# Routing of a mixture of experts emitted among the next step's attention, with four expert tiles left over from step to step

## The chip, the cores and the metric

The kernel runs on one core of a Trainium2 chip. The core has a matrix engine (TensorE, PE below), three engines for elementwise work (VectorE, DVE; ScalarE, ACT; GpSimd, POOL), a queue engine that here only starts transfers (SyncE, SP), and 16 DMA engines. Each engine works through its own list of instructions in order, and an instruction that has to wait holds everything behind it on that engine. The metric is the time of one execution on the device, in microseconds.

## The reference

Two layers over an image of 2 x 56 x 56 positions with 256 channels, all in float32.

- Layer 0: group norm, then attention of every position over its 7 x 7 neighbourhood (8 heads), added to the input.
- Layer 1: layer norm, then a linear attention along the 3136 tokens of each image with running sums, added; then layer norm and a mixture of 8 experts, of which each token uses two, added.

The part that matters here, in short:

```python
t = t + _L1_attn_ref(_ln_t(t), ...)
xf = _ln_t(t).reshape(-1, 256)
probs = softmax(xf @ gate_w + gate_b)              # 8 experts
top2_vals, top2_idx = top_k(probs, 2)              # weights of the two best
for e in range(8):
    h = gelu(xf @ W1[e] + b1[e])                   # 256 -> 512
    y = h @ W2[e] + b2[e]                          # 512 -> 256
    t = t + cw[:, e] * y                           # cw is 0 unless e is among the two best
```

## The kernel before

Layer 0 takes the first 485 us and is not touched. Layer 1 walks over the tokens in 14 steps (`NST`), each of 448 tokens: 224 of each image, as four blocks of 112. For every step `s` there are three sequences of work, written as Python generators that emit a few instructions and then yield. One yield is called a turn.

- `before_pairs(s)` loads the step's tokens into `x`, normalises and transposes them (`norm_T`), projects q, k and v and makes the rows of gates and softmax weights. Its scans and four reciprocals on 16 x 224 values are DVE work.
- `attention(s)` makes the running sums: `p_gt` is its first matmul, `sc`, `zz` and `po` the core, `p_out` the last projection, and the result is added to `x`. In the kernel before it ends with `route(s, x)`.
- `route` normalises `x` into `xs` and transposes it (`pt_x` from `xs`), multiplies by the gate weights (`p_gate`), takes softmax and the rank of each expert on DVE, and writes `taken`. After that come six empty turns (`PAUSE`). Then `p_n` counts the tokens of each expert with two small matmuls; DVE makes the row numbers `rowi`; POOL writes the tokens to their experts' regions in `xs_d` in device memory with eight indirect transfers (scatters), each after the one before. `listed(s)` writes the list of full tiles. Last, `p_cw` and `p_b` add the experts' output biases to `x`, and POOL writes `x` to `out`.

Besides these runs one generator `experts()` for the whole layer. A tile is 256 tokens of one expert. `fetch` reads the tile's list entry on SP and loads its tokens (`xg`, from `xs_d`) and the expert's weights (`wj`, 1 MB), two tiles ahead (`ahead = 2`). `gather` transposes the tokens (`pt_g`), `hidden` makes 512 hidden values (`p_h`, then gelu on ACT), and `results` multiplies back (`p_y`), scales (`ye`), and adds the rows into `out` with an indirect transfer that accumulates. The rows' numbers come from a cast of a column of `xg` (`rows_e`). A tile takes `per_tile` = 7 turns; there are 56 (`NX`). `sure(s)` is the number of tiles that are full after step `s` whatever the input: 0, 0, 3, 7, 10, 14, 17 and so on to 42.

`together(main, *others)` sets the order: after every turn of the main generator it takes as many turns of the others as keep them at their share of the main one's expected turns. The main one is `attention(s)`, routing included (47 turns); the others are the tiles that the step before made sure, less two, and `before_pairs(s + 1)`. After the last step two more tiles run, then the list is closed, and the remaining 18 tiles run alone.

The instructions of each engine follow this order closely; a scheduler moves some of them forward, among them loads on SP and the cast `rows_e`. Data in device memory is tracked by tensor: a fetch waits for the scatters emitted before it, a scatter for the fetches before it, and an accumulation into `out` for the one before.

Matmul results go to PSUM; pool `l_mm` has six buffers that all these products share. `x`, `xs`, `xg` and `wj` come from pool `p3` with three buffers each, `ye` and `rows_e` from `p6` with six. `general` is a second form of the layer for other inputs, which does not run here.

Of the kernel before, what the change touches and what calls it, by code (L numbers as in the profile page):

```python
# [14 lines left out]
F32 = mybir.dt.float32  # L15
# [12 lines left out]
C = 256  # L28
# [12 lines left out]
TT = 112  # L41
BLK = 448
BT = BLK // NB
NST = L // BT
NTI = BLK // TT
# [12 lines left out]
NX = (2 * NB * L - NE) // SL + NE  # L58
TOK, CWC = C, C + 1
ROW = C + 16  # L60
PAUSE = 6


def sure(s):

    return max(0, -((NE * (SL - 1) - 2 * BLK * (s + 1)) // SL))
# [88 lines left out]
def hybrid_kernel(ctx: ExitStack, tc: tile.TileContext, t: dict, out: bass.AP):  # L155
# [170 lines left out]
    with (  # L326
# [36 lines left out]
        for n in range(2):  # L363
            o = p1.tile([TT, 2, NH, HD + 1], F32, name=f"values{n}")
# [169 lines left out]
        for i in range(NT):  # L534
            going, done = project(i + 2) if i + 2 < NT else iter(()), 0
# [103 lines left out]
    def layer_1(general):  # L639
        with (  # L640
# [3 lines left out]
            p1 = steps.enter_context(tc.tile_pool(name="l1", bufs=1))  # L644
            p2 = steps.enter_context(tc.tile_pool(name="l2", bufs=2))
            p3 = steps.enter_context(tc.tile_pool(name="l3", bufs=2 if general else 3))
            p6 = steps.enter_context(tc.tile_pool(name="l6", bufs=2 if general else 6))
            ps_a = steps.enter_context(tc.tile_pool(name="l_acc", bufs=1, space=PSUM))

# [75 lines left out]
            def before_pairs(s):  # L725

                nonlocal m_prev, s_prev, g_prev
                x = p3.tile([TT, NTI, C], F32, tag="x", name="x_acc")
                for b in range(NB):
                    nc.sync.dma_start(  # L730
                        out=x[:, b * 2 : (b + 1) * 2, :],
# [48 lines left out]
                at = 0  # L780
# [187 lines left out]
            def attention(s):  # L968
                x, q, k, v, gl, cf = ready.pop(s)
                yield from (sums_general if general else sums_plain)(s, q, k, v, gl, cf)  # L970

                for i in range(NTI):
                    ps = ps_m.tile([TT, C], F32, tag="mm", name="p_out")
                    for g in range(NG):
                        nc.tensor.matmul(
                            ps,
                            lhsT=q[:, g, i * TT : (i + 1) * TT],
                            rhs=wo1[:, g, :],
                            start=g == 0,
                            stop=g == NG - 1,  # L980
                        )
                    nc.vector.tensor_tensor(x[:, i, :], ps, x[:, i, :], ALU.add)
                    yield
                yield from route(s, x)

            def sums_general(s, q, k, v, gl, cf):

# [154 lines left out]
                    nc.vector.tensor_tensor(qg, spread(cf, g, rep), own, ALU.mult)  # L1142
                    yield

            def route(s, x):


                nonlocal n_prev, c_prev, at_prev
                xs = p3.tile([TT, NTI, ROW], F32, tag="xs", name="xs")
                nc.gpsimd.memset(xs[:, :, CWC + NE :], 0.0)  # L1150
                xT = yield from norm_T(x, "xT_f", p1, xs)
# [29 lines left out]
                ahead = p1.tile(full, F32, tag="ahead", name="ahead")  # L1181
# [22 lines left out]

                taken = p2.tile([TT, NTI, NE], F32, tag="taken", name="taken")
                nc.vector.tensor_single_scalar(taken, rank, 1.5, ALU.is_lt)  # L1206
                for _ in range(PAUSE):
                    yield
                pn = ps_m.tile([P, 2, NTI, NE], F32, tag="mm", name="p_n")
                flat = taken.rearrange("p i e -> p (i e)")  # L1210
                nc.tensor.matmul(  # L1211
# [9 lines left out]
                n = p2.tile([P, NTI + 1, NE], F32, tag="n", name="n")  # L1221
# [131 lines left out]
            def fetch(j):  # L1353

                ent, k = listed_at.pop(j)
                known = "the lists hold rows of the regions and experts alone"
                row = nc.values_load(
                    ent[0:1, 0, k : k + 1],
                    engines=[mybir.EngineType.SP],
                    min_val=0,  # L1360
                    max_val=NE * RG,
                    skip_runtime_bounds_check_because=known,
                )
                exp = nc.values_load(
                    ent[0:1, 1, k : k + 1],
                    engines=[mybir.EngineType.SP],
                    min_val=0,
                    max_val=NE - 1,
                    skip_runtime_bounds_check_because=known,
                )  # L1370
                xg = p3.tile([P, SL // P, ROW], F32, tag="xg", name="xg")
                nc.sync.dma_start(
                    out=xg, in_=xs_d[bass.ds(row, SL), :].rearrange("(u p) c -> p u c", p=P)
                )
                wj = p3.tile([P, NG * FF + NF * C + NF], F32, tag="wj", name="wj")
                nc.sync.dma_start(
                    out=wj, in_=t["we"][bass.ds(exp, 1)].rearrange("o p c -> (o p) c")
                )
                return xg, wj

            def gather(xg):

                pt = ps_h.tile([P, NG, SL], F32, tag="mm", name="pt_g")
                for u in range(SL // P):
                    for g in range(NG):
                        nc.tensor.transpose(  # L1386
                            pt[:, g, u * P : (u + 1) * P], xg[:, u, g * P : (g + 1) * P], ident
                        )
                xT = p2.tile([P, NG, SL], F32, tag="xT_g", name="xT_g")
                nc.scalar.copy(xT, pt)  # L1390
                return xT

            def hidden(xT, wj):
                w1 = wj[:, : NG * FF].rearrange("p (k f) -> p k f", k=NG)
                b1 = wj[:, NG * FF + NF * C :]
                hT = p2.tile([P, NF, SL], F32, tag="hT", name="hT")
                for f in range(NF):
                    ph = ps_h.tile([P, SL], F32, tag="mm", name="p_h")
                    for k in range(NG):
                        nc.tensor.matmul(  # L1400
                            ph,
                            lhsT=w1[:, k, f * P : (f + 1) * P],
                            rhs=xT[:, k, :],
                            start=k == 0,
                            stop=k == NG - 1,
                        )
                    nc.scalar.activation(hT[:, f, :], ph, AF.Gelu, bias=b1[:, f : f + 1])  # L1407
                    yield
                return hT
# [41 lines left out]
            def experts():  # L1451


                fetched = {k: fetch(k) for k in range(ahead)}
                yield
                xT = gather(fetched[0][0])
                for k in range(NX):
                    if k + ahead < NX:
                        fetched[k + ahead] = fetch(k + ahead)
                    xg, wj = fetched.pop(k)  # L1460
                    hT = yield from hidden(xT, wj)
                    if k + 1 < NX:
                        xT = gather(fetched[k + 1][0])
                    yield
                    yield from results(k, hT, xg, wj)
# [8 lines left out]
            def together(main, *others):  # L1474


                going = [[gen, n, 0, wait * main[1]] for gen, n, wait in others]
                for done, _ in enumerate(main[0], 1):
                    for o in going:
                        while o[2] < o[1] and o[2] * (main[1] - o[3]) < (done - o[3]) * o[1]:  # L1480
                            next(o[0], 0)
                            o[2] += 1
                for gen, n, at, _ in going:
                    for _ in range(at, n):
                        next(gen, 0)
                return done
# [1 line left out]

            ready, listed_at = {}, {}
            ahead = 1 if general else 2
            tiles = experts()
            per_tile = NF + 1 + SL // P
            n_before = sum(1 for _ in before_pairs(0)) + 1
            n_step = 70
            for s in range(NST):
                n_tiles = max(0, sure(s - 1) - ahead) - max(0, sure(s - 2) - ahead)
                begin = n_tiles and sure(s - 2) <= ahead
                if begin:  # L1500
                    next(tiles)
                with_it = [(tiles, n_tiles * per_tile, 0.5 if begin else 0)]
                if s + 1 < NST:
                    with_it.append((before_pairs(s + 1), n_before, 0))
                n_step = together((attention(s), n_step), *with_it)
            for _ in range(ahead * per_tile):
                next(tiles)


            behind = p1.tile([P, NE], I32, tag="behind", name="behind")  # L1510
# [21 lines left out]
    with tc.If(flag != 0):  # L1532
        layer_1(False)
    with tc.If(flag == 0):  # L1534
        layer_1(True)
# [56 lines left out]
```

## Time and profile before

The median of three runs is 1860.25 us (1853.78 to 1864.68). The profile is of one execution of 1865.8 us.

| stretch | us | what runs |
|---|---|---|
| 0 to 515.3 | 515.3 | layer 0 and the first `before_pairs` |
| 515.3 to 697.7 | 182.4 | steps 0 to 2, no tiles |
| 697.7 to 770.3 | 72.6 | step 3, one tile |
| 770.3 to 1548.4 | 778.1 | steps 4 to 12, 32 tiles |
| 1548.4 to 1590.3 | 41.9 | attention of step 13 |
| 1590.3 to 1640.3 | 50.0 | routing of step 13, tiles |
| 1640.3 to 1865.8 | 225.5 | last tiles |

A step is cut here from one `p_gt` on PE to the next. In the timeline each line has the start, the time from the first start to the last end of the merged instructions, engine, line, operation, output and inputs, and how many (a float32 matmul shows as two). What stands in square brackets is the idle time of the engine just before and the instruction that ended it. A line of the windows has the stretch, its length, then busy time and number of instructions of PE, PE's weight loads, DVE, ACT and POOL, the clock granted to PE, the busy share of the DMA engines and GB/s.

### The profile page before, as it was taken

Reading aid. Unit: us, or ns where it says so; the run is one execution under the profiler, and the core shown is the slowest. Engines: PE = TensorE matmul, PEld = TensorE weight load, DVE = VectorE, ACT = ScalarE, POOL = GpSimd, SP = SyncE. Lnnn points to the kernel's source line nnn. Section 1 sums busy time; section 2 is a strip of 40 time slices with the busy share of each in tenths; the row PEclk is TensorE's granted clock in tenths of the full one; section 3 lists DMA queues with packets and bytes.
Section 4 is the critical chain, followed back from the end, with each engine's and each line's share of the span. In section 5 each row is a group of like instructions: output and inputs, shape, how many; then the busy total and the mean of one; then the engine's idle time right before and its main releaser. Section 6 shows DMA issues by size and latency. Waiting matters only on the chain. (4 is left out here: it accounts for less than half of the span.)

```text
span 1865.8 us, 28574 instructions
## 1 busy us (share of the span) xinstructions
PE 1504.1 (81%) x10840; PEld 1075.6 (58%) x10840; DVE 936.4 (50%) x2787; ACT 626.3 (34%) x1125; POOL 448.5 (24%) x496
## 2 busy tenths in 40 slices
PE   0899999999487778898798879888887888778781
PEld 0466776789254445565465556556565656666670
DVE  3455566654466775655637373746465464411110
ACT  0233433432333233443325333433344241322220
POOL 2123333332101101213131322213131313322232
PEclk9989999975688779899899989898899899989885
DMA  7345554452101103234242414232333324276542
GB/s 227 119 147 168 161 152 145 150 164 85 41 1 41 31 11 127 47 107 109 61 115 63 116 45 126 62 92 71 106 75 98 105 61 109 65 238 170 137 106 27
DMA packets 110786, 190.35 MB, mean 102 GB/s; under 512 B 17674, under 2 KB 92290, under 8 KB 103460
## 3 DMA queue, kind: packets, MB, share of 16 engines
q1 hardware_dynamic: 74612, 128.27, 21.7%
q0 software_dynamic: 32560, 54.55, 13.2%
q10 hardware_dynamic: 3456, 5.51, 0.9%
q8 instruction: 89, 1.46, 0.3%
q14 instruction: 69, 0.57, 0.1%
HBM read 131.52 MB, written 56.73 MB: 101 GB/s over the span
## 5 line engine op out<-in xcount | busy, mean ns | idle before, releaser
L1440 POOL DMA_INDIRECT out<-ye,rows_e x112 | 175.3, 1565 | 635.7 <-DVE ye L1439 206.8
L1400 PE MATMUL p_h<-xT_g,wj 128*128 128x256 f32 x896 | 242.1, 411 | 14.0 <-DVE ye L1439 9.6
L1431 PE MATMUL p_y<-wj,hT 128*128 128x256 f32 x896 | 230.8, 409 | 1.1 <-DVE ye L1439 1.1
L1407 ACT ACTIVATE hT<-p_h,wj 128x256 f32<-128x256 f32 x224 | 105.7, 474 | 351.2 <-PE p_h L1400 317.2
L1400 PEld LDWEIGHTS p_h<-xT_g,wj 128*128 128x128 f32 x896 | 175.8, 204 | 52.6 <-issue 18.2
L1431 PEld LDWEIGHTS p_y<-wj,hT 128*128 128x128 f32 x896 | 178.0, 206 | 38.4 <-issue 9.5
L1246 POOL DMA_INDIRECT xs_d<-xs,rowi x112 | 107.6, 961 | 321.6 <-DMA xs_d<-xs,rowi 129.5
L503 ACT ACTIVATE ex<-ex 98x1024 f32<-98x1024 f32 x98 | 103.8, 1060 | 228.0 <-DVE ex L497 219.2
L1415 DVE CAST rows_e<-xg 128x2 int32<-128x2 f32 x56 | 9.5, 169 | 301.2 <-DMA xg<-xs_d 202.6
L497 DVE TENSOR_TENSOR ex<-sc,bias 98x1024 f32<-98x1024 f32 x98 | 119.7, 1221 | 66.9 <-PE sc L488 65.3
L512 PE MATMUL po<-vw,ex 98*64 98x33 f32 x3136 | 129.2, 240 | 5.8 <-DMA vw<-v_d 5.8
L512 PEld LDWEIGHTS po<-vw,ex 98*64 98x64 f32 x3136 | 117.2, 157 | 23.7 <-DMA vw<-v_d 7.1
L488 PE MATMUL sc<-qb,kc 64*98 64x128 f32 x1568 | 130.0, 311 | 0.0
L488 PEld LDWEIGHTS sc<-qb,kc 64*98 64x98 f32 x1568 | 106.0, 187 | 40.5 <-issue 28.6
L916 PE MATMUL sc<-qh,v 128*112 128x448 f32 x224 | 112.3, 598 | 0.0
L924 DVE TENSOR_TENSOR qv<-sc,upto 112x448 f32<-112x448 f32 x112 | 69.2, 622 | 72.1 <-PE sc L916 70.7
L1439 DVE TENSOR_SCALAR ye<-p_y,cws 128x256 f32<-128x256 f32 x112 | 52.6, 478 | 80.8 <-PE p_y L1431 57.3
L1211 PE MATMUL p_n<-taken,every 112*128 112x32 f32 x28 | 8.2, 383 | 89.9 <-DVE taken L1206 89.9
L315 POOL TENSOR_TENSOR xo<-xo,xq 128x256 f32<-128x256 f32 x49 | 35.6, 727 | 181.4 <-DVE xo L309 173.3
L1386 PE MATMUL pt_g<-ident,xg 128*128 128x128 f32 x224 | 39.4, 304 | 41.1 <-DVE ye L1439 26.2
L954 PE MATMUL po<-qv,kt 112*32 112x112 f32 x896 | 45.7, 277 | 30.9 <-DVE qv L924 30.9
L888 ACT COPY qh<-q 32x448 f32<-32x448 f32 x112 | 63.0, 562 | 2.2
(234 smaller groups left out, 2543.3 us busy)
## 6 DMA issues: line engine op xcount, KB each, us to landing
wj<-in_we SPq DMA_DIRECT2D x56, 1026.0 KB
vw<-v_d SPq DMA_DIRECT2D x196, 101.1 KB
xg<-xs_d SPq DMA_DIRECT2D x56, 272.0 KB
v_d<-values POOLq DMA_DIRECT2D x28, 231.0 KB, 3.7
xq<-in_x SPq DMA_DIRECT2D x98, 64.0 KB
q_d<-evq POOLq DMA_DIRECT2D x28, 224.0 KB, 3.0
qb<-q_d SPq DMA_DIRECT2D x56, 112.0 KB
x_d<-xo POOLq DMA_DIRECT2D x98, 64.0 KB, 3.1
```

Of the source, the lines that this page charges most:

```text
L488: nc.tensor.matmul(sc[:KN, p, b, k], lhsT=keys(i, j, k, b, rows, g), rhs=qb[rows, g, :, b, j * QN : (j + 1) * QN], start=True, stop=True,)
L497: nc.vector.tensor_tensor(ex[:KN], sc[:KN].rearrange("n p b k h q -> n p b (k h q)"), tables[kind][:KN, g].unsqueeze(2).to_broadcast(wide) ...
L503: nc.scalar.activation(ex[:KN], ex[:KN], AF.Exp)
L512: nc.tensor.matmul(po[b * QN : (b + 1) * QN, hh, :], lhsT=ex[:KN, p, b, k, h, :], rhs=vw[:KN, b, k, hh * (HD + 1) : (hh + 1) * (HD + 1)], ...
L888: nc.scalar.copy(qh[hp, h, :], qg[hp])
L916: nc.tensor.matmul(sc, lhsT=vg[:, i * TT : (i + 1) * TT], rhs=qh[:, :, i * TT : (i + 1) * TT], start=True, stop=True,)
L924: nc.vector.tensor_tensor(qv, sc, upto.unsqueeze(1).to_broadcast([TT, 4, TT]), ALU.mult)
L1246: nc.gpsimd.indirect_dma_start(out=xs_d[:, :], out_offset=bass.IndirectOffsetOnAxis(ap=rowi[:, c, i : i + 1].bitcast(U32), axis=0), in_=xs ...
L1400: nc.tensor.matmul(ph, lhsT=w1[:, k, f * P : (f + 1) * P], rhs=xT[:, k, :], start=k == 0, stop=k == NG - 1,)
L1407: nc.scalar.activation(hT[:, f, :], ph, AF.Gelu, bias=b1[:, f : f + 1])
L1431: nc.tensor.matmul(py, lhsT=hT[:, f, u * P : (u + 1) * P], rhs=w2[:, f, :], start=f == 0, stop=f == NF - 1,)
L1440: nc.gpsimd.indirect_dma_start(out=out[:, :], out_offset=bass.IndirectOffsetOnAxis(ap=rows[:, u : u + 1].bitcast(U32), axis=0), in_=y, in_ ...
```

## The change

Routing becomes a sequence of its own. `attention(s)` now ends with the last addition to `x` (27 turns) and leaves `x` in `routed`; during step `s + 1`, `together` takes the 17 turns of `route(s)` over the first 0.6 of the attention's turns. Of the six empty turns one is left. Its purpose is to have the routing's chain through DVE run beside attention, not after it.

As the list of step `s` is now written during step `s + 1`, four tiles (`wait`) and not two are left over from step to step, so that a tile is not fetched before it is listed. The look-ahead of fetches stays at two. The first tile starts in step 4 and not in step 3. After the last step, routing of step 13 is the main sequence and the four tiles left run beside it, spread over 1.5 times its turns. `x` gets a pool of its own with three buffers. Lines after the first change are shifted by up to six in the changed kernel: `p_n` is at L1213, `rows_e` at L1417, `p_h` at L1402, the accumulation at L1442.

```diff
-PAUSE = 6
...
+            p4 = steps.enter_context(tc.tile_pool(name="l4", bufs=2 if general else 3))
...
-                x = p3.tile([TT, NTI, C], F32, tag="x", name="x_acc")
+                x = p4.tile([TT, NTI, C], F32, tag="x", name="x_acc")
...
-                yield from route(s, x)
+                routed[s] = x
+                if general:
+                    yield from route(s)
...
-            def route(s, x):
+            def route(s):
...
+                x = routed.pop(s)
...
-                for _ in range(PAUSE):
-                    yield
+                yield
...
-                going = [[gen, n, 0, wait * main[1]] for gen, n, wait in others]
-                for done, _ in enumerate(main[0], 1):
+                going = [[gen, n, 0, a * main[1], b * main[1]] for gen, n, a, b in others]
+                done = 0
+                for _ in main[0]:
+                    done += 1
                     for o in going:
-                        while o[2] < o[1] and o[2] * (main[1] - o[3]) < (done - o[3]) * o[1]:
+                        while o[2] < o[1] and o[2] * (o[4] - o[3]) < (done - o[3]) * o[1]:
...
+            wait = 1 if general else 4
...
-            n_step = 70
+            n_step, n_route = 45, 17
             for s in range(NST):
-                n_tiles = max(0, sure(s - 1) - ahead) - max(0, sure(s - 2) - ahead)
-                begin = n_tiles and sure(s - 2) <= ahead
-                if begin:
-                    next(tiles)
-                with_it = [(tiles, n_tiles * per_tile, 0.5 if begin else 0)]
+                n_tiles = max(0, sure(s - 1) - wait) - max(0, sure(s - 2) - wait)
+                begin = n_tiles and sure(s - 2) <= wait
+                with_it = []
+                if s and not general:
+                    with_it.append((route(s - 1), n_route, 0, 0.6))
                 if s + 1 < NST:
-                    with_it.append((before_pairs(s + 1), n_before, 0))
+                    with_it.append((before_pairs(s + 1), n_before, 0, 1))
+                with_it.append((tiles, n_tiles * per_tile + (begin > 0), 0.5 if begin else 0, 1))
                 n_step = together((attention(s), n_step), *with_it)
-            for _ in range(ahead * per_tile):
-                next(tiles)
+            together((() if general else route(NST - 1), n_route), (tiles, wait * per_tile, 0, 1.5))
```

## The prediction

> **What bounds the kernel now.** I read the engine table first, then the windows cut at the step boundaries, then the waits of TensorE (PE), and last the timelines around each wait. The chain of waits is little help: it covers the last 9% of the span.
>
> The table of engines names one engine that could be the bound, PE; VectorE (DVE) is at half.
>
> ```profile
> PE 1504.1 (81%) x10840; PEld 1075.6 (58%) x10840; DVE 936.4 (50%) x2787; ACT 626.3 (34%) x1125; POOL 448.5 (24%) x496
> ```
>
> Layer 1 begins its first attention at 515.3 us (first `p_gt`), and each later `p_gt` starts a step. A window from one `p_gt` to the next gives (length, then PE busy, PE weight loads, DVE) for step 1, with no expert tile, and steps 4 and 5, with four and three:
>
> ```profile
> 577.90:637.40 59.50, 46.07 (x263) 28.74 (x264) 41.61 (x121) 19.95 (x36) 3.94 (x5) 0.84 0.03 9
> ...
> 770.30:855.10 84.80, 76.17 (x407) 52.51 (x406) 49.43 (x180) 35.71 (x61) 21.97 (x20) 0.94 0.35 98
> 855.10:941.90 86.80, 69.88 (x373) 48.55 (x371) 47.40 (x162) 29.76 (x53) 19.58 (x18) 0.88 0.30 80
> ```
>
> Steps 4 to 12 last 778.1 us and keep PE busy for 663.0, so PE stands 115, or 12.8 a step; a step without tiles stands 13 to 15. The routing makes most of that. Its group of the page, and the timeline of PE in one step:
>
> ```profile
> L1211 PE MATMUL p_n<-taken,every 112*128 112x32 f32 x28 | 8.2, 383 | 89.9 <-DVE taken L1206 89.9
> ```
>
> ```profile
> 1430.75 0.32 PE L718 MATMUL pt_x<-ident,xs 112*128 112x112 f32 x1 [1.43 <-DVE xs L707]
> ...
> 1436.63 1.65 PE L1155 MATMUL p_gate<-gw,xT_f 128*112 128x8 f32 x16
> 1438.13 2.84 PE L1400 MATMUL p_h<-xT_g,wj 128*128 128x256 f32 x12
> 1449.40 0.64 PE L1211 MATMUL p_n<-taken,every 112*128 112x32 f32 x2 [8.44 <-DVE taken L1206]
> ...
> 1450.23 2.05 PE L1400 MATMUL p_h<-xT_g,wj 128*128 128x256 f32 x4
> ```
>
> From the gate's end (1438.1) to `p_n` DVE needs 11.3 us; PE has 2.8 us of other work queued ahead of `p_n`, then stands 8.44 and runs the next `p_h` x4 in 2.05 instead of 1.03. In the other kind of step 5.7 us of 10.5 are filled and 4.4 to 4.6 stand. Mean over 14 steps: 89.9/14 = 6.4.
>
> The other waits in a step are `pt_x` on the normalised tokens (1.43 or 2.61, 32.2 in all), `p_b` (0.6), and `po` on `qv` and `p_h` on `ye` (30.9 and 9.6 in all). The last two come from DVE itself being held:
>
> ```profile
> 1307.37 0.41 SPq L1372 DMA_DIRECT2D xg<-xs_d  x1
> ```
>
> ```profile
> 1310.78 0.17 DVE L1415 CAST rows_e<-xg 128x2 int32<-128x2 f32 x1 [10.39 <-DMA xg<-xs_d]
> ```
>
> The eight scatters of the routing run one after another from 1281.2 to 1307.4, the next fetch `xg` waits for them, and a small cast that reads it stands in DVE's order ahead of attention.
>
> Tail: after step 13's attention (1590.3) 275.5 us follow. PE waits at 1640.3 for the fetch of tile 38, which needs the last scatter (issued 1634.5); from there 38 serial accumulations into `out` take 5.5 us each to the end, against 3.7 us of PE for half a tile (7.34 a tile, 1670.28 to 1677.62).
>
> ```profile
> 1640.26 1.09 PE L1386 MATMUL pt_g<-ident,xg 128*128 128x128 f32 x4 [11.86 <-DMA xg<-xs_d]
> ```
>
> **What the skill says.** The Trainium skill, "Perfetto Trace Analysis", section "Optimization Strategy", advises to interleave stretches with different limits and to find what each gap on the bounding engine waits for; the change does the first, and the lines above are the second. "TensorE: Matmul & The Clock Gate", section "What's actually happening", says that about 3.4 us of idleness halves PE's clock for about as long. The trace agrees: after the 8.44 us gap 2.05 against 1.03 us. So a gap over some 4 us costs about 2 more, inside "busy".
>
> **The change, part by part.** The order of instructions of both kernels, which the build fixes, tells what lies between a producer and its wait.
>
> *The routing of step s moves into step s+1.* Nothing is added to PE: routing is 7 us of it (transposes 1.7, gate 1.65, `p_n` 0.7, `p_cw` 0.55, `p_b` 2.3). The waits change:
> - `p_n`. In the new order DVE has, between gate and `taken`, the 14 routing operations (3.5 us together by their rows), Exp with its table load (1.5), two `qv` (0.62 each) and in one kind of step a `ye` (0.48), but none of the 1.53 us reciprocals that `before_pairs` puts there now: 6.7, with latencies about 7.7. PE has queued ahead of `p_n`: 2 `p_h`, 2 `sc`, a transpose group, `zz` and `po` (6.4 us), or the same with a `p_y` and a `pt_g` in place of one `p_h` (7.9). Left: 0 to 1.5, I take 1. Dropping five of six pauses costs nothing for that reason.
> - `pt_x`. It now stands at the head of the step: behind the last `p_out` only a `p_y` and `p_gt` (2.5 us), or `p_gt` alone (0.6). The chain is 4.3 to 4.6 us now (last `p_out` 1426.5 or 1513.7 to `pt_x`); DVE has the next step's statistics mixed in (two to four of 0.42 us), so about 6. Left: 3.5 and 5.4, mean 4.5, up from 2.
> - Scatters and fetch. In a three-tile step the fetch needs all eight scatters: 3 us from `p_n` to `rowi`, 26 for the scatters (as now) plus about 2.5 for accumulations queued between them, 3.4 for the fetch: 35 after `p_n`, where PE has 33 us of work before DVE meets the cast. In a four-tile step a first fetch comes after two scatters, the third scatter waits for it to land, and the cast for the second fetch is ready about 43 us after `p_n` (3 to `rowi`, 9 for two scatters and the accumulation between them, 5 for that fetch, 21 for six scatters and one accumulation, 5 to land and fetch) while PE has 28 and, with six PSUM buffers, some 7 more. Left: 1 and 7, mean 4, as now (40.5 us over ten steps). Behind the cast stand `qv`, the `x_acc` additions and `q`; PE waits for them when its buffers are full.
> - `p_b` 0.6, as now. Sum of idleness a step: 4.5 + 1 + 4 + 0.6 = 10.
>
> *Busy time.* PE's 663.0 us in steps 4 to 12 less 32 tiles of 7.34 (235) is 47.6 a step; with one long gap fewer I take 46.
>
> *Four tiles left over.* With `sure()` = 3, 7, 10, 14 ... tiles start in step 4 rather than 3; steps 4 to 12 hold 31 instead of 32, step 13 three, four run with routing 13. The tail of 18 tiles and its accumulations stay. The new order of Pool's queue keeps four or five accumulations among the last eight scatters, and tile 38's transposes still stand ahead of tile 37's results: those 50 us are bound by scatter and fetch, as now, and the extra tile work lies in PE's 11.86 us gap. I add 3.
>
> *The separate pool for `x`* keeps three buffers: nothing. The load of `x` still waits for the output of three steps before; its new place, late in the step before its use, leaves about 8 us.
>
> Sum, before to after:
> - step 0: 62.6 to 47.5 (routing gone, 7 of PE and 8 of waits): -15
> - steps 1, 2: 59.9 each to 57 (46.6 + 10): -6
> - step 3: 72.6 to 57 (no tile): -15.5
> - steps 4 to 12: 778.1 to 9 x 46 + 31 x 7.34 + 90 = 731.5: -46.5
> - step 13 to its last `p_out`: 41.9 to 23.5 + 7 + 22 + 10 = 62.5: +20.5
> - rest: +3
>
> -59.5, so 1860.25 - 59.5 = **1801 us**.
>
> **Rivals.**
> 1. *All waits hidden.* DVE's queue order is kinder than my sums and 5 us a step stand: 13 steps x 5 = 65 less, 1736. For: DVE is busy only 48 of 86 us. Against: `pt_x` has little work ahead in every step.
> 2. *The wait only moves.* `p_n` goes, but `pt_x` and the casts grow to 14 a step: 13 x 4 = 52 back, 1853. For: `pt_x` and scatter are chains through several engines, untouched.
> 3. *Slower.* In every step with tiles the cast holds DVE for the whole 43 - 28 = 15 us and PE with it, `pt_x` stays at 5: 20 a step with the rest, 10 more than mine in ten steps: 1901. Against: six PSUM buffers, and now 10.4 us of held DVE cost PE only 2 to 5.
> 4. *Tail-bound:* if accumulation already limited the steps, a shorter step would return in the tail. Seven accumulations of 4.5 and eight scatters of 2.9 us are 55 of 75 us: small, counted under 2.
>
> **Chances.** My forecast 0.63; rival 1 0.15; rivals 2 and 4 0.12; rival 3 0.10. The idleness of 10 could be 7 or 13: 39 either way. The range leaves out most of 3 and the far half of 1: 1742 to 1856. Faster by over 0.5% (below 1851): 0.63 + 0.15 + 0.03 = 0.81; within: 0.08; slower: 0.11.
>
> **What would show it.** Wait of `p_n` on `taken` under 25 us in all (89.9 now); of `pt_x` on `xs` 50 to 70 (32.2 now); steps 4 to 12 mean 81; the last step's attention to the end within 8 us of 275.5; longest casts on `xg` 10 to 15 us in four-tile steps. I am wrong if steps 4 to 12 stay at 86, if `p_n` still stands over 4 us a step, or if the end after `p_out` grows by more than 15.

## The result, and the profile after

The changed kernel takes **1780.01 us** (median of 4 runs, 1774.15 to 1805.72), the kernel before 1862.47 (4 runs, 1853.78 to 1870.11). The ratio is 0.955, 95% interval 0.949 to 0.961: 73 to 96 us less. Two later measurements of the same pair gave 0.965 (0.955 to 0.976) and 0.968 (0.947 to 0.989), so some 60 to 85 us is what the change is worth. The forecast was 59.5 less.

TensorE's granted clock drifts between runs: the stretch up to layer 1's first attention, the same instructions in every kernel here, took 484.9 to 518.5 us in the profiles. The ratios are therefore of those runs of either kernel that are nearest its fastest, and I compare stages from that attention on (first `p_gt`, to the end of the span). Three profiles of the unaltered changed kernel give 1274.6, 1280.6 and 1296.2 us; this spread is the noise of one profile.

The engine table of the profile after, and the windows between `p_gt`s for step 1, steps 4 to 6, and from step 13 to its last `p_out`. Columns: length; busy time and count of PE, PE weight loads, DVE, ScalarE (ACT) and GpSimd (POOL); granted clock, DMA share, GB/s.

```profile
PE 1476.4 (83%) x10840; PEld 1055.9 (59%) x10840; DVE 936.1 (53%) x2787; ACT 660.2 (37%) x1157; POOL 448.7 (25%) x496
```

```profile
551.00:608.80 57.80, 50.27 (x261) 30.28 (x261) 38.16 (x114) 20.52 (x35) 9.24 (x11) 0.82 0.11 33
...
728.70:821.10 92.40, 72.93 (x375) 50.52 (x374) 55.55 (x195) 35.56 (x60) 15.62 (x15) 0.85 0.32 100
821.10:891.80 70.70, 67.42 (x371) 45.84 (x370) 43.65 (x144) 33.75 (x56) 20.44 (x19) 0.95 0.38 98
891.80:976.60 84.80, 76.37 (x407) 54.23 (x406) 50.48 (x181) 38.93 (x64) 21.55 (x19) 0.94 0.37 98
...
1449.20:1508.20 59.00, 52.72 (x304) 38.65 (x304) 27.28 (x111) 14.91 (x27) 17.81 (x17) 0.97 0.40 106
```

The three-tile steps gained most: 83.6 to 86.8 us before, 69.5 to 77.1 in the three profiles of the changed kernel. The four-tile steps from step 6 on moved less, 87.3 to 90.2 before, 81.5 to 87.2 now, and PE still stands 8.4 us in the one shown. Step 4, where tiles begin, is long, with 19.5 us of idle PE. Stage by stage:

| stage | before | after | change | forecast |
|---|---|---|---|---|
| ahead of the first `p_gt` (not altered) | 515.3 | 506.3 | -9.0 | 0 |
| step 0 | 62.6 | 44.7 | -17.9 | -15 |
| steps 1 and 2 | 119.9 | 116.4 | -3.5 | -6 |
| step 3 | 72.5 | 61.3 | -11.2 | -15.5 |
| steps 4 to 12 | 778.1 | 720.5 | -57.6 | -46.5 |
| step 13 to its last `p_out` | 42.0 | 59.0 | +17.0 | +20.5 |
| rest | 275.4 | 272.7 | -2.7 | +3 |

From the first `p_gt` on that is -75.9 (-69.9 and -54.3 with the other two profiles): PE stands 60.0 us less (268.6 to 208.6) and is busy 15.9 less (1081.9 to 1066.0). The -9.0 ahead of it is drift.

PE's waits (who waited, for what; total, times, longest), two of them before and then those of the profile after:

```profile
PE pt_x L718 <- DVE xs L707: 32.2, 14, 3.3
PE po L954 <- DVE qv L924: 30.9, 13, 5.5
```

```profile
PE pt_x L718 <- DVE xs L707: 52.0, 14, 7.3
...
PE pt_g L1388 <- DVE ye L1441: 24.1, 7, 4.3
...
PE p_out L975 <- DVE q L965: 12.9, 7, 3.0
PE p_y L1433 <- ACT hT L1409: 11.1, 4, 3.5
...
PE p_n L1213 <- DVE taken L1209: 7.1, 5, 2.3
...
PE po L954 <- DVE qv L924: 2.7, 4, 1.6
```

The wait that the change was for, `p_n` on `taken`, fell from 89.9 to 7.1 us; `po` on `qv` fell from 30.9 to 2.7. `pt_x` on `xs`, at the head of the step now, rose by 19.8. The rest are small ones, spread over several lines.

### The profile page after: what moved, and what is told of

Its sections match the earlier page's. It is cut to its first block, busy times and chain, and to the rows that moved or that the text cites. A ratio compares the mean times of both kernels' runs of the same rounds, so it can differ in the third digit from the quotient of the medians.

```text
span 1780.9 us, 28613 instructions
## 1 busy us (share of the span) xinstructions
PE 1476.4 (83%) x10840; PEld 1055.9 (59%) x10840; DVE 936.1 (53%) x2787; ACT 660.2 (37%) x1157; POOL 448.7 (25%) x496
## 4 chain that ended last, share of the span: by engine, by line
PE 34%; DMA 15%; DVE 15%; issue 5%; ACT 3%; SPq 1%; POOL 1%; DVEq 0%; POOLq 0%; ACTq 0%
DMA out<-ye,rows_e 7%; PE p_qkv L750 7%; PE p_h L1402 6%; PE p_y L1433 6%; DMA xg<-xs_d 5%; PE sc L916 4%; DMA xs_d<-xs,rowi 2%; PE pt_x L718 2%; DVE lst L696 2%; PE p_gate L1158 1%; PE p_b L1267 1%; DVE ye L1441 1%; PE po L954 1%; DVE cf L852 1%; PE p_out L975 1%
## 5 line engine op out<-in xcount | busy, mean ns | idle before, releaser
L1442 POOL DMA_INDIRECT out<-ye,rows_e x112 | 176.9, 1579 | 493.9 <-DVE ye L1441 126.0
L1402 PE MATMUL p_h<-xT_g,wj 128*128 128x256 f32 x896 | 239.5, 403 | 4.4 <-DMA wj<-in_we 4.4
L1433 PE MATMUL p_y<-wj,hT 128*128 128x256 f32 x896 | 229.2, 405 | 12.2 <-ACT hT L1409 11.1
L1402 PEld LDWEIGHTS p_h<-xT_g,wj 128*128 128x128 f32 x896 | 174.0, 202 | 54.6 <-issue 33.0
L1417 DVE CAST rows_e<-xg 128x2 int32<-128x2 f32 x56 | 9.7, 174 | 243.5 <-DMA xg<-xs_d 147.7
L511 PE MATMUL po<-vw,ex 98*64 98x33 f32 x3136 | 124.0, 235 | 7.4 <-DMA vw<-v_d 7.3
L511 PEld LDWEIGHTS po<-vw,ex 98*64 98x64 f32 x3136 | 112.0, 150 | 24.5 <-DMA vw<-v_d 9.0
L487 PEld LDWEIGHTS sc<-qb,kc 64*98 64x98 f32 x1568 | 98.2, 175 | 41.6 <-issue 27.7
L487 PE MATMUL sc<-qb,kc 64*98 64x128 f32 x1568 | 121.1, 296 | 1.4 <-DVE ex L496 1.4
L760 DVE SCALAR_TENSOR_TENSOR pd<-p_qkv,bq,k 128x448 f32<-128x448 f32 x28 | 19.1, 684 | 107.0 <-ACT q L758 107.0
L718 PE MATMUL pt_x<-ident,xs 112*128 112x112 f32 x112 | 27.6, 347 | 52.0 <-DVE xs L707 52.0
L975 PE MATMUL p_out<-L_woT,q 128*112 128x256 f32 x224 | 59.6, 391 | 13.1 <-DVE q L965 12.9
```

Source lines behind the costliest of these rows:

```text
L487: nc.tensor.matmul(sc[:KN, p, b, k], lhsT=keys(i, j, k, b, rows, g), rhs=qb[rows, g, :, b, j * QN : (j + 1) * QN], start=True, stop=True,)
L511: nc.tensor.matmul(po[b * QN : (b + 1) * QN, hh, :], lhsT=ex[:KN, p, b, k, h, :], rhs=vw[:KN, b, k, hh * (HD + 1) : (hh + 1) * (HD + 1)], ...
L975: nc.tensor.matmul(ps, lhsT=q[:, g, i * TT : (i + 1) * TT], rhs=wo1[:, g, :], start=g == 0, stop=g == NG - 1,)
L1402: nc.tensor.matmul(ph, lhsT=w1[:, k, f * P : (f + 1) * P], rhs=xT[:, k, :], start=k == 0, stop=k == NG - 1,)
L1433: nc.tensor.matmul(py, lhsT=hT[:, f, u * P : (u + 1) * P], rhs=w2[:, f, :], start=f == 0, stop=f == NF - 1,)
L1442: nc.gpsimd.indirect_dma_start(out=out[:, :], out_offset=bass.IndirectOffsetOnAxis(ap=rows[:, u : u + 1].bitcast(U32), axis=0), in_=y, in_ ...
```

## The experiments

Each kernel's total is a median beside the kernel before on the same chip. "From `p_gt`" is the stretch from the first `p_gt` to the end in its one profile, "busy" and "idle" are PE's in it.

| kernel | us | before, same chip | from `p_gt` | busy | idle |
|---|---|---|---|---|---|
| before (first profile) | 1862.5 | - | 1350.5 | 1081.9 | 268.6 |
| four left over alone | 1876.1 | 1867.0 | 1370.9 | 1084.9 | 286.0 |
| filler ahead of `p_n` | 1838.6 | 1862.9 | 1327.8 | 1115.7 | 212.1 |
| after (first profile) | 1780.0 | 1862.5 | 1274.6 | 1066.0 | 208.6 |
| after, second and third time | 1775.8; 1798.8 | 1862.9; 1866.2 | 1280.6; 1296.2 | 1068.1; 1077.3 | 212.5; 218.9 |
| six empty turns kept | 1781.3 | 1867.0 | 1260.4 | 1041.0 | 219.4 |
| routing packed into 0.33 | 1841.2 | 1867.0 | 1339.8 | 1091.4 | 248.4 |
| routing from 0.08 on | 1776.9 | 1867.0 | 1276.2 | 1065.4 | 210.8 |
| first tiles fetched early | 1783.9 | 1862.9 | 1271.7 | 1067.9 | 203.8 |
| routing spread over 0.8 | 1789.8 | 1862.9 | 1281.4 | 1048.7 | 232.7 |
| cast on GpSimd | 1748.7 | 1866.2 | 1242.9 | 1064.2 | 178.7 |
| six turns and early fetch | 1767.1 | 1866.2 | 1245.3 | 1042.6 | 202.7 |
| these two and the cast | 1712.4 | 1866.2 | 1205.6 | 1034.5 | 171.1 |

### Is it the routing's place, or the four tiles left over?

The kernel before, with only `wait`:

```diff
+            wait = 1 if general else 4
-                n_tiles = max(0, sure(s - 1) - ahead) - max(0, sure(s - 2) - ahead)
-                begin = n_tiles and sure(s - 2) <= ahead
+                n_tiles = max(0, sure(s - 1) - wait) - max(0, sure(s - 2) - wait)
+                begin = n_tiles and sure(s - 2) <= wait
...
-            for _ in range(ahead * per_tile):
+            for _ in range(wait * per_tile):
```

> The kernel before with four tiles left over from step to step and routing still at the end of its own step. If the move of the routing makes the gain, this one gains little: two tiles leave the steps and run in the 11.9 us in which PE waits for the fetch of tile 38, so 1845 to 1865 us; p_n waits on taken for 85 to 100 us in all as before. If the four tiles left over make it, 1800 us or less.

Measured 1876.13 us (1846.19 to 1876.69), the kernel before 1866.95 on the same chip; the expectation of no gain held, a little above its upper end. From `p_gt` on it is 20.4 longer: step 3 lost a tile (72.5 to 60.2), but what follows the last `p_out` grew from 275.4 to 306.6. PE's waits are those of before, 89.8 us on `taken` included:

```profile
PE p_n L1211 <- DVE taken L1206: 89.8, 14, 9.0
...
PE po L954 <- DVE qv L924: 35.5, 11, 7.0
```

So the four tiles are no gain; the 9 us of the medians and the 20 of the profiles that they cost here are no more than the noise of one profile. The opposite half, routing moved with fewer tiles left, wasn't tried: a tile would be fetched ahead of its list. Nor was the separate pool for `x` tried alone.

### How much of the old gap was only clock?

The kernel before, with matmuls whose result nothing reads in three of the six empty turns ahead of `p_n`:

```diff
-                for _ in range(PAUSE):
+                warm = None if general else ps_m.tile([P, BLK], F32, tag="mm", name="p_warm")
+                for n in range(PAUSE):
+                    if not general and n % 2:
+                        for g in range(NG):
+                            nc.tensor.matmul(
+                                warm, lhsT=wo1[:, g, :P], rhs=xT[:, g, :], start=g == 0, stop=g == NG - 1
+                            )
                     yield
```

> The kernel before, with three pairs of matmuls more in the routing of each step, in its empty turns ahead of p_n, whose result nothing reads: some 5 us of TensorE work in a gap that stands 6.4 us on average. Nothing of the order of the other work changes. Theory (part of the gap's cost is that TensorE comes back at half its clock, about 2 us a gap): the wait of p_n falls from 89.9 to 20 to 35, but only the clock is gained: 14 to 28 us less than the kernel before, 1835 to 1850. Rival (the granted clock depends on something else, or the dummies delay p_n where VectorE was earlier): 1860 to 1885.

```profile
PE po L954 <- DVE qv L924: 48.6, 15, 5.3
...
PE p_n L1217 <- DVE taken L1206: 25.8, 9, 5.1
```

`p_n`'s wait fell to 25.8, as expected; `po` on `qv`, 30.9 before, rose to 48.6. The medians fell from 1862.94 (23 runs) to 1838.55 (20 runs), inside the range expected, and from `p_gt` on by 22.7; but the ratio is 0.9935 (0.9866 to 1.0004), which doesn't exclude zero. In the profile the filler is 69.8 us of PE, and PE's real work fell from 1081.9 to 1115.7 - 69.8 = 1045.9. The trace also tells when the clock was halved. Half of the time that PE is busy in such spells, from `p_gt` on, is what the clock costs: 100.5 us before, 72.3 with the filler, and 80.1, 82.8 and 92.4 in the three profiles of the changed kernel. That a clock kept up is worth some 8 to 25 us of the change's gain is likely, not settled; the other two thirds or more is work that now runs where PE stood.

### Six empty turns or one

The changed kernel with six turns again (`n_route` 22 for 17):

```diff
-                yield
+                for _ in range(6):
+                    yield
                 pn = ps_m.tile([P, 2, NTI, NE], F32, tag="mm", name="p_n")
```

> The changed kernel with all six empty turns ahead of p_n (22 turns of routing in the same 0.6 of a step). My account: p_n already waits only 7 us in all, so more work ahead of it (about 16 us a step in place of 7) gains at most those 7, and the scatters start some 9 us later: 1773 to 1792 us. A rival holds that the later scatters hold the fetch, the casts and then PE: 1800 us or more.

The total of 1781.27 (1772.28 to 1786.20) is in the range expected. The stages are not the same, though: steps 5 to 12 take 610.9 us against 628.1, 628.4 and 637.0, step 13 to its last `p_out` 52.0 against 59.0 to 64.7, and what follows 284.9 against 272.7 to 280.6. With the early fetch added, below, steps 5 to 12 again take 611.9. Steps 5 to 12 in the second profile of the changed kernel, then with six turns:

```profile
827.00:1455.40 628.40, 567.63 (x3105) 397.39 (x3104) 378.56 (x1305) 291.43 (x484) 163.15 (x145) 0.96 0.36 95
```

```profile
829.10:1440.00 610.90, 552.87 (x3106) 391.31 (x3105) 386.30 (x1308) 292.98 (x484) 164.46 (x144) 0.96 0.37 98
```

From `p_gt` on PE is idle at least as long as in the changed kernel (219.4) and busy 25 to 36 less. So the turn count does matter, by 14 to 36 us from `p_gt` on, through busy time. The total hides it, in part because the stretch ahead of `p_gt` took 516.9 us in this profile. The mean clock is no higher, as the two lines show, but its low spells fall more where PE stands anyway: the clock costs 65.7 us of busy time here, against 80.1 to 92.4, which is 14 to 27 of the 25 to 36. Why they fall so with this order, and where the other 10 come from, the runs don't settle.

### Routing packed, delayed or spread

One number of the line `with_it.append((route(s - 1), n_route, 0, 0.6))` each: `0, 0.33`; `0.08, 0.6`; `0, 0.8`.

> The changed kernel with routing's 17 turns over the first 0.33 of the attention and not 0.6; four tiles left over as before. Ahead of p_n PE has 3 to 5 us of other work in place of 5 to 8, so my account gives p_n a wait of 2 to 4 us a step, 30 to 50 in all, and 1795 to 1815 us. Rival: scatters that start earlier free the fetch and the casts and win as much back: 1775 to 1785.

> The changed kernel with routing spread from 0.08 to 0.6 of the attention and not from 0. PE then has about 6 us of other work between the last p_out and pt_x where it had 0.3 to 2.3, and p_n gets 1 to 3 us more. My account: the wait of pt_x on xs goes from 52 us to under 10, with it some slow clock after gaps over 4 us: 1730 to 1750 us. Rival: the wait only moves, to the casts on xg and to q, since the chain of scatters ends later: 1772 to 1785.

> The changed kernel with the routing of a step spread over the first 0.8 of the next attention's turns instead of 0.6. Packing it into 0.33 made the steps some 60 us longer in all, nearly all of it in TensorE's waits on VectorE work of attention that came to stand behind routing (p_n, sc, p_h, kt: some 60 us). Theory (the thinner routing is spread, the less attention's operations wait behind it on VectorE): pt_x on xs falls from 52 to 25 to 40, the stretch from the first attention on is 8 to 20 us shorter, the whole 1760 to 1772. Rival (0.6 is thin enough and the later scatters hold the fetch and with it VectorE longer): waits for rows_e rise, the whole 1780 to 1800.

**Packed**: 1841.21 us (1819.63 to 1860.06), much slower than either theory. `pt_x` did not change (50.0). What grew is PE's waits on DVE:

```profile
PE p_n L1213 <- DVE taken L1209: 25.0, 14, 3.2
...
PE sc L916 <- DVE pd L760: 16.3, 4, 5.1
PE p_h L1402 <- DVE pd L777: 12.5, 4, 3.8
...
PE sc L916 <- DVE kt L894: 6.7, 4, 2.8
PE p_gate L1158 <- ACT xT_f L721: 6.7, 6, 1.4
```

Of these only `p_n` was there in the changed kernel, at 7.1. They are 60 us more, of which other waits gave some back (`p_y` on `hT`, 11.1 in the changed kernel, is gone): idle PE rose by 30 to 40 and busy time by 14 to 25 from `p_gt` on. My theory had counted `p_n` alone. Attention's own `pd` and `kt` came to stand behind routing in DVE's order, and the matmuls that need them with it.

**Delayed**: 1776.93 us (1751.13 to 1795.65), the rival's side. The wait aimed at did fall, from 52.0 to 13.9, and came back elsewhere:

```profile
PE zz L936 <- ACT vt L908: 15.2, 7, 3.2
PE p_y L1433 <- DVE qv L924: 14.0, 4, 4.1
PE pt_x L718 <- DVE xs L707: 13.9, 8, 9.9
...
PE zz L936 <- DVE lmv L697: 7.5, 3, 3.6
```

The three others are new, 36.7 us against the 38.1 gained. From `p_gt` on the kernel is where the changed one is, at 1276.2.

**Spread over 0.8**: `pt_x` rose from 50.7 to 78.8 where I had it fall, three-tile steps became shorter and four-tile steps longer, and the sum stayed (1281.4 against 1280.6 on the same chip):

```profile
1193.40:1285.80 92.40, 77.24 (x406) 54.53 (x406) 54.74 (x184) 40.34 (x65) 24.28 (x22) 0.89 0.37 100
1285.80:1354.80 69.00, 64.93 (x372) 45.15 (x371) 42.07 (x147) 34.45 (x57) 16.31 (x16) 0.98 0.33 84
```

The rival was right for the four-tile steps (91.6 to 95.1 against 81.5 to 87.2): the list comes later, and DVE stands 267 us in the cast instead of 250. Three placements of the same routing, and none is clearly better than 0 to 0.6 in its total.

### The first tiles, earlier

```diff
                 with_it = []
+                if begin:
+                    next(tiles)
...
-                with_it.append((tiles, n_tiles * per_tile + (begin > 0), 0.5 if begin else 0, 1))
+                with_it.append((tiles, n_tiles * per_tile, 0.5 if begin else 0, 1))
```

(The tiles keep to the second half of step 4, other than the expectation says; only the first two fetches move to its start.)

> The changed kernel, but the first two tiles are fetched at the start of step 4 and the tiles of that step are spread over all of it, not over its second half. In the changed kernel step 4 lasts 92.4 us with 19.5 us of idle TensorE, against 84.4 for the other four-tile steps. Theory (step 4 is long because its tiles are squeezed into the second half behind two first fetches of 5.9 and 4.4 us): step 4 falls to 80 to 85, the whole to 8 to 12 us less, 1765 to 1775. Rival (the fetch at the start meets the last eight scatters of the routing, the cast on it holds VectorE, and the loss only moves): step 4 stays at 90 or more, whole within 4 us.

```profile
725.10:804.40 79.30, 67.78 (x376) 46.89 (x375) 52.51 (x190) 35.53 (x60) 15.53 (x15) 0.94 0.30 84
```

Step 4 takes 79.3 us against 92.3 in the changed kernel on the same chip; from `p_gt` on 1271.7 against 1280.6. The theory held for the stage. The total, 1783.85 beside 1775.76 and above the 1775 expected, doesn't show it: the gain is smaller than the drift of the clock.

> The changed kernel unaltered, as the base for the other three runs on this chip. 1770 to 1790 us. The stretch up to the first attention of layer 1, which no kernel here alters, took 501.5 to 518.5 us in the profiles so far, so I compare from that point on: 1274.6 us in the first profile of this kernel; expected 1260 to 1280 again.

That run gave 1775.76 us (1768.69 to 1794.62), and 1280.6 from `p_gt` on, just above what I expected.

### The cast that stands in DVE's order

In a four-tile step of the changed kernel DVE meets three casts that wait for a fetch, and 4 us after the last of them PE waits its longest but one in the step. Timelines of DVE and of PE:

```profile
925.36 0.17 DVE L1417 CAST rows_e<-xg 128x2 int32<-128x2 f32 x1 [2.96 <-DMA xg<-xs_d]
...
948.38 0.17 DVE L1417 CAST rows_e<-xg 128x2 int32<-128x2 f32 x1 [4.57 <-DMA xg<-xs_d]
...
955.39 0.17 DVE L1417 CAST rows_e<-xg 128x2 int32<-128x2 f32 x1 [4.93 <-DMA xg<-xs_d]
```

```profile
896.80 0.77 PE L718 MATMUL pt_x<-ident,xs 112*128 112x112 f32 x2 [4.29 <-DVE xs L707]
...
959.30 0.70 PE L1433 MATMUL p_y<-wj,hT 128*128 128x256 f32 x2 [3.41 <-ACT hT L1409]
```

No wait of PE names the cast. From the waits alone one would price it at 3 us a step at most.

```diff
-                nc.vector.tensor_copy(rows, xg[:, :, TOK : TOK + 1].rearrange("p u o -> p (u o)"))
+                nc.gpsimd.tensor_copy(rows, xg[:, :, TOK : TOK + 1].rearrange("p u o -> p (u o)"))
```

> The changed kernel unaltered once more, as the base for the other three runs on this chip: 1765 to 1795 us. From the first attention of layer 1 on it took 1274.6 and 1280.6 us in its two profiles; expected 1270 to 1285.

> The changed kernel with the small cast of the fetched row numbers (rows_e on xg) on GpSimd, not on VectorE. It stands 197 us in VectorE's order in the changed kernel, ahead of attention's operations. Theory (part of TensorE's remaining waits, p_out on q 13, p_y on hT 11, pt_g on ye 24 in all, come from VectorE held by the cast): these fall by 10 to 25 in all, and the stretch from the first attention on lasts 1250 to 1268. Rival (PSUM buffers already cover what the cast holds, and GpSimd, which issues the scatters, is now held instead): 1272 to 1290.

**1748.69 us** (1740.03 to 1757.98), ratio to before 0.947 (0.936 to 0.959); the changed kernel on this chip 1798.83 (1774.50 to 1813.57), and 1296.2 from `p_gt` on, above what I expected, at a low clock (0.891). From `p_gt` on 1242.9, better than the theory's 1250 to 1268. A four-tile and a three-tile step:

```profile
889.90:967.90 78.00, 72.85 (x408) 52.17 (x407) 50.84 (x176) 38.87 (x64) 20.19 (x21) 0.98 0.39 105
967.90:1039.60 71.70, 68.36 (x372) 46.99 (x371) 44.86 (x149) 34.07 (x57) 22.77 (x23) 0.93 0.37 96
```

Steps 6, 8, 10 and 12 take 78.2 us on average against 84.1, 84.8 and 84.6 in the three profiles of the changed kernel, steps 5, 7, 9 and 11 70.4 against 72.9, 72.4 and 74.7. So the held cast costs 6 us in a four-tile step and 2 to 4 in a three-tile one. Of PE's waits, `p_y` on `hT` (11 us) is gone and `p_out` on `q` fell from 12.9 to 9.1; `pt_g` on `ye` went, and `p_y` on `ye` came with 23.7. PE stands 178.7 us from `p_gt` on where it stood 208.6 to 218.9, and is busy as long as before (1064.2). On GpSimd, busy 26% of the time, the cast takes 0.49 us instead of 0.17 and waits in its turn; the steps are shorter all the same.

### The best of it

Six empty turns in all routings but the last, and the early fetch:

```diff
-                yield
+                for _ in range(6 if s < NST - 1 else 1):
+                    yield
...
-            n_step, n_route = 45, 17
+            n_step, n_route = 45, 22
...
-            together((() if general else route(NST - 1), n_route), (tiles, wait * per_tile, 0, 1.5))
+            together((() if general else route(NST - 1), n_route - 5), (tiles, wait * per_tile, 0, 1.5))
```

> The changed kernel with six empty turns ahead of p_n again in all routings but the last, and with the first two tiles fetched at the start of step 4. Each alone changed one thing in its profile: the six turns made steps 5 to 12 last 610.9 us against 628.1 and 628.4 (but what follows the last p_out 12 longer), the early fetch made step 4 last 79.3 against 92.4. If the two add up: steps 4 to 12 in 690 to 697 us, from the first attention to the end 1240 to 1255, 15 to 30 us less than the changed kernel on this chip, 1740 to 1765 in all. If they don't (the shorter steps of the six turns were the clock of one profile): steps 5 to 12 at 625 to 635, 1265 to 1272 from the first attention on.

> The same two edits together with the cast on GpSimd. With the six turns pt_x stands up to 12.5 us on xs at the step's head, in the stretch after the last p_out too, where I suppose that VectorE is held by a cast. Theory: with the cast off VectorE that wait falls from 73.7 in all to under 40, what follows the last p_out from 284.9 to 270 to 275, and from the first attention on 1222 to 1245 remain. Rival (pt_x waits for the chain through its own operations, whatever else VectorE does): pt_x stays at 65 to 80, and the time is that of the two edits without it within 5 us, or longer where GpSimd's scatters come later.

The two edits give 1767.07 us (1749.91 to 1774.98); from `p_gt` on 1245.3, steps 4 to 12 691.5: in the stages they add up, as the first branch said; the total is just above its 1765. With the cast on GpSimd as well: **1712.37 us** (1688.65 to 1732.34), ratio to before 0.925 (0.908 to 0.942), the fastest kernel here. From `p_gt` on it is 1205.6, shorter than the theory's 1222 to 1245 and 39.7 less than without the cast's move; alone that move gave 31.7 to 53.3. A three-tile and a four-tile step of it:

```profile
1229.70:1296.60 66.90, 63.44 (x372) 44.26 (x371) 45.20 (x150) 34.18 (x57) 19.34 (x19) 1.00 0.38 101
1296.60:1373.90 77.30, 72.63 (x407) 52.33 (x406) 50.98 (x173) 39.10 (x64) 24.06 (x24) 0.96 0.38 102
```

Two numbers of my expectation failed: `pt_x` fell only to 54.9, not under 40, and the stretch after the last `p_out` stayed at 280.8. So the cast was a quarter of `pt_x`'s 73.7 (72.7 with the two edits), and the rest is likely its own chain, which lies between the theory and its rival. The end of the kernel is what none of these edits touched.

## Why the prediction was right

- **`p_n`**: forecast 1 us a step left, measured 0.5 (7.1 in all). Right, and the main term.
- **Step 0, step 13, the rest**: -15, +20.5, +3 forecast, -17.9, +17.0, -2.7 measured. Right; that the tail stays tied to scatter and fetch as before shows in its 50.0 us from the last `p_out` to tile 38's transposes, 53.3 now.
- **Steps 1 to 3**: a little smaller than forecast, -14.7 for -21.5.
- **Steps 4 to 12**: forecast 731.5, measured 720.5, 720.7 and 725.2. Two terms of the sum: busy 641.5 forecast, 640.7 to 646.8 measured; idle 90 forecast, 74.5 to 80 measured. The busy term was right for its reason too: beside the tile less (7.3), the clock costs 33.4 to 40.9 us of these steps' busy time, 49.6 before. The idle term was the mis-sized one.
- **`pt_x`** is the part of it that shows in the waits: 3.5 and 5.4 us forecast, 1.15 to 3.1 measured in the three-tile steps and 4.3 in the four-tile steps of the first profile. The sum over the kernel, 52.0, lies in the 50 to 70 forecast only because the heads of steps 2 to 4, with no tile beside them, wait 7.2 to 7.3; that the sum came right is in part luck.
- **The held cast**: 1 and 7 us forecast, 2 to 4 and 6 shown by the cast's move to GpSimd, in part as busy time. The mean of 4 was right. The form was not: I had one cast of 10 to 15 us a step, and the profiles have several, in steps 5 to 12 of 6.3 at most in the first and 7.5 in the others. In steps 6, 8 and 10 three successive ones sum to 12.2 to 15.3.
- **"Dropping five of six pauses costs nothing"** is the step that failed. Nothing had to wait for `p_n`, as I had worked out, and yet the order with six turns is 14 to 36 us shorter from `p_gt` on, by PE's busy time. I had costed the turns by one wait, but they shift every later routing instruction among attention's.
- **What I did not see**: step 4's two first fetches, for which PE waits 5.9 and 4.4 us in the second half of the step; they make it 92.4, where the other four-tile steps take 84. It hid some of what the idle term had too much.
- Rival 1 had 5 us a step left standing; it is 8.3 to 8.9 in steps 4 to 12. Rival 4's return in the tail didn't come: what follows the last `p_out` is 272.7 to 280.6, 275.4 before. Rival 2, the wait that only moves, describes the delayed routing exactly, and not the change. Rival 3's mechanism is real, at 6 us a four-tile step and not 15.

## What to carry to other kernels

A chain through several engines that stands at the end of a step is worth moving beside the next step's independent work: PE's 89.9 us on `taken` nearly vanished, for tiles left over whose own price, 9 to 20, is within the noise. What is then left are in-order queues: look for a tiny instruction that waits for a DMA ahead of real work on a busy engine, even if no wait of the bounding engine names it, and give it to the engine that needs its result anyway; here a 0.17 us cast cost some 40 (31.7 to 53.3). Price each step of such a plan by moving one thing at a time, since a wait taken away at one place (38 us of `pt_x`) can come back at three others.

## What the runs showed of the hardware

A short stand of PE can be followed by a loss well above its length. Both stretches below are of the second profile of the changed kernel, two three-tile steps with the same work, each with the same 1.63 us wait of `po` on `qv` (at 1355.16 and 1195.39). Windows of 2 us:

```profile
1353.00:1355.00 2.00, 0.54 (x4) 0.34 (x2) 2.00 (x5) 1.99 (x4) 0.00 (x0) 1.00 0.97 352
1355.00:1357.00 2.00, 1.56 (x19) 0.88 (x20) 1.94 (x6) 1.94 (x5) 0.00 (x0) 0.75 0.97 278
1357.00:1359.00 2.00, 2.00 (x5) 1.17 (x6) 2.00 (x9) 0.83 (x3) 0.78 (x1) 0.50 0.05 17
```

```profile
1193.00:1195.00 2.00, 0.76 (x5) 0.53 (x3) 2.00 (x5) 1.97 (x4) 0.00 (x0) 1.00 0.96 334
1195.00:1197.00 2.00, 1.34 (x19) 0.82 (x20) 1.94 (x5) 1.94 (x5) 0.00 (x0) 1.00 0.96 277
1197.00:1199.00 2.00, 2.00 (x9) 1.33 (x9) 2.00 (x8) 1.50 (x4) 0.20 (x1) 1.00 0.28 79
```

In the first the granted clock, the third number from the end, halves and stays so for 10 us; in the second it stays at 1.00. The steps take 76.0 and 72.0 us (the longer one also has a low spell of 3.4 us at its head). After a wait of 0.94 us (`p_b`, at 854.06 of the first profile after) the clock was low for some 7 us as well. Summed in steps of 1 us over steps 5 to 12, each such drop lost 1.7, 3.4 or 5.1 us of full clock, which is one, two or three spells of 3.4 us at half. In each of the 14 profiles the low spells of steps 4 to 12, 211 in all, start on one even grid of 3.413 us, to within 0.002. That agrees with the Trainium skill, "TensorE: Matmul & The Clock Gate", section "What's actually happening", which has a free-running window of some 3.4 us. That section, and my prediction after it, have an idle window as the condition; here windows idle in part were enough. Counted on the grid, in steps 4 to 12 of all 14 profiles: each of the 150 full-clock windows in which PE was idle for over 1.97 us was followed by half the clock, none of the 2133 with under 0.61 was, and 52 of the 275 between were.

Both waits shown are of that middle kind, and each lies whole in one window of the grid (1.65 and 1.63 us idle, from 1352.58 and 1192.16 on). So neither the length of the wait nor a split of it by the grid tells the two apart. The matmuls beside it may count: `p_b`, by the wait of 0.94 us, is 8*112 where `p_h` is 128*128. No run here tests that.
